# A Perceiver layer on one core: a written order for the prologue, helpers moved off VectorE, and a shorter last routing

## The chip, the cores and the metric

The kernel runs on one core of a Trainium2 chip. Its engines are TensorE (PE: matmuls and transposes), VectorE (DVE), ScalarE (ACT: activation functions from loaded tables), GpSimd (POOL) and SyncE (SP: issues DMAs). Each has its own in-order instruction stream; they synchronise by semaphores. The metric is the device time of one execution in microseconds. Kernel before: median 3076.52 us of three runs (3073.73 to 3076.61).

## The reference

Two batches of 512 tokens by 512 features (x), and two contexts of 8192 rows by 384 features. All arithmetic is in fp32.

```python
x = x + cross_attention(layernorm(x), ctx, mask, Wq, Wk, Wv, Wo)   # 16 heads of 32, 8192 keys, softmax
x = x + self_attention(layernorm(x), ...)   # 16 heads, causal, scores from amplitude and phase:
#   amp = softplus(x @ Wamp.T), normed by its root mean square in each head; phi = pi * tanh(x @ Wphi.T)
#   scores = (q_amp cos(q_phi) . k_amp cos(k_phi) + q_amp sin(q_phi) . k_amp sin(k_phi)) / sqrt(32) * exp(scale)
x = x + ffn(layernorm(x))                   # 16 experts, each token goes to its top 2
#   probs = softmax(x @ w_router); top_k(probs, 2); each expert takes 64 tokens of a batch at most, in the
#   order: all first choices by token, then all second choices; later ones are dropped
#   y = sum over the two choices of prob * w_proj(silu(w_gate x) * w_fc x)
```

An equal score goes to the lower expert number in the choice.

## The kernel before

**Cross-attention** is most of the time. Keys are taken in chunks of 1024 (8 a batch, 16 in all), heads in four groups of four. One chunk and one group is a *step*: 64 steps, each of eight *rounds* (one for each 128 keys, `kt`). A round on PE is: the scores of four heads for the row maxima of a later step (`heads_max`, L375, `LEAD` = 12 rounds ahead), the same scores with keys on partitions for the exponentials (`heads_exp`: L388 and the bias product L407), and one further piece: in even rounds the products with the values of the two rounds before (`values`, L440), in odd ones a piece of the keys two steps on (`k_half`) or a v tile of the next chunk (`v_tile`), both through `columns` (L166: 128 columns as four products of 32, side by side on the array). DVE takes the four maxima of 512 scores (L397), and adds products to the accumulator (L453, L455). ACT takes the four exponentials (L409), copies v tiles, the maxima as rows (`max_rows`, L431). POOL adds the exponentials of the step up to one tile (`es`, L570), from which PE makes the sums of the softmax (L467). When the running maximum moves, `shrink` scales the accumulator (L462, L463).

**Before the steps**, `prepare` (L239 to L328) loads the weights and the mask, computes layer norm of x for both batches (`norm_pieces`, L93 to L127), transposes it (`turn`, L139 and the copy L140), projects the queries (L310, 128 columns wide) and gathers the first masked column of the context for what the code calls the first keys (L283, L321). Its operations are left to a scheduler, and so is their order. Then a written order (`tc.manual_schedule()`, L493) holds: the k halves of steps 0 and 1, twelve rounds of maxima with the eight v tiles of chunk 0, row maxima, and the loop over steps (L514 to L584). `sa_tables` (L951 to L967), small tables for the self-attention, are made in step 1.

**When a batch ends** (step 32 is the first of batch 1), the last group's accumulator is divided by its sums in `divide` (L476 reciprocal, L477 product) on DVE, and `finish_tile` (L479 to L484) multiplies each of four token tiles by Wo and adds it to x. For other groups the product of `divide` is on POOL.

**During the last six steps**, `xattn_tail` (L881) gives out pieces of the self-attention of batch 0: norm (steps 58, 59), transposes, phases, amplitudes. One of them goes into each round: PE's into a free PSUM bank (`fill`), DVE's at the round's end (`fill_dve`). Tanh (L1235) and Sin (L1031) of the phases, and the square roots and logarithm of the amplitudes, are on ACT. The self-attention and the experts form a second `manual_schedule` (L1355); what lies between the two written blocks has its place by dependencies.

**Routing** (`route`, L645 to L760) gives 20 pieces: statistics and norm of the tokens, storing them to DRAM, transposes, router product (L679), softmax and two choices (L686 to L704), running counts of tokens for each expert (L710 to L725), rank and slot (L730 to L733), `hit` and `whose` (L734, L741), and a product that turns them into the list of tokens of each expert (L750, L753). For batch 0 they are spread over the self-attention of batch 1. For batch 1 they stand at the end (L1343 to L1350): after the last output tile nothing else is left for PE. Then `experts`: for each of 16, POOL fetches 128 rows by an indirect DMA (L767), PE transposes, expands (L788) and contracts (L805); results go to DRAM and are gathered back for each token (L833).

Of the kernel before, what the change touches and what calls it, by code (L numbers as in the profile page):

```python
# [42 lines left out]
def perceiver_kernel(ctx: ExitStack, tc: tile.TileContext, a, out: bass.AP):  # L43
# [33 lines left out]
    for b in range(B):  # L77
        nc.sync.dma_start(xs[:, b * TB : (b + 1) * TB, :], x_in[:, b * TB : (b + 1) * TB, :])
# [12 lines left out]
    lnp = ctx.enter_context(tc.tile_pool(name="ln", bufs=2))  # L91

    def norm_pieces(b, keep=None):  # L93
# [27 lines left out]

        class Tiles(list):
# [3 lines left out]
        pieces = [lambda i=i: stats(i) for i in range(TB)] + [scale] + [lambda i=i: normed(i) for i in range(TB)]  # L126
# [49 lines left out]
    def cross_attention(tail):  # L176

        with ExitStack() as st:
# [17 lines left out]
            def load_chunk(i):  # L196
                b, c = chunks[i]
                t = [m4("ctx", (P, CH)) for j in range(NC)]
                src = a["ctxT"][b].rearrange("(c p) k -> p c k", p=P)
                for j in range(NC):  # L200
                    nc.sync.dma_start(t[j], src[:, j, c * CH : (c + 1) * CH])
                m8 = sm.tile([P, CH], U8, tag="m8", name="m8")
                row = a["mask_BxS2_bf1"][b : b + 1, c * CH : (c + 1) * CH]
                nc.sync.dma_start(m8, row.to_broadcast([P, CH]))
                ctx_tiles[i], mask_tiles[i] = t, m8
# [3 lines left out]
            for w, n in ((wk, "Wk"), (wv, "Wv")):  # L209
                for j in range(NC):  # L210
                    nc.scalar.dma_start(w[j], a[f"L0_xattn_{n}"][j * P : (j + 1) * P, :])
            wo = b8("wo")
            nc.scalar.dma_start(wo, a["L0_xattn_Wo"].rearrange("(c p) d -> p c d", p=P))
            load_chunk(0)
# [24 lines left out]
            def prepare():  # L239

                with tc.tile_pool(name="xa_q", bufs=1) as qp:
                    wq = b8("wq")
                    nc.scalar.dma_start(wq, a["L0_xattn_Wq"].rearrange("(c p) d -> p c d", p=P))
                    mc8 = qp.tile([P, B, M // P], U8, name="mc8")
                    nc.gpsimd.dma_start(mc8, a["mask_BxS2_bf1"].rearrange("b (p n) -> p b n", p=P))

                    left_i = qp.tile([P, M // P], I32, name="left_i")
                    nc.gpsimd.iota(left_i, pattern=[[-1, M // P]], base=M, channel_multiplier=-(M // P))
                    left = qp.tile([P, M // P], F32, name="left")
                    nc.vector.tensor_copy(left, left_i)  # L250
                    val = qp.tile([P, B, M // P], F32, name="val")
                    nc.vector.tensor_tensor(
                        val, left.unsqueeze(1).to_broadcast([P, B, M // P]), mc8, ALU.mult
                    )
                    vm = qp.tile([P, B], F32, name="vm")
                    nc.vector.tensor_reduce(vm, val, AX.X, ALU.max)
                    pm = bank()
                    pf = bank()
                    nc.tensor.transpose(pm[:B, :P], vm, ident)
                    vb = qp.tile([B, 1], F32, name="vb")  # L260
                    nc.vector.tensor_reduce(vb, pm[:B, :P], AX.X, ALU.max)
                    dg = qp.tile([B, B], F32, name="dg")
                    nc.vector.tensor_scalar(dg, ident[:B, :B], vb, None, ALU.mult)
                    nc.tensor.matmul(pf[:, :B], ones[:B, :], dg, start=True, stop=True)
                    first = qp.tile([P, B], F32, name="first")
                    nc.vector.tensor_scalar(first, pf[:, :B], -1.0, float(M), ALU.mult, ALU.add)
                    nc.vector.tensor_scalar_min(first, first, M - 1.0)
                    anyb = qp.tile([P, B], F32, name="anyb")
                    nc.vector.tensor_scalar_min(anyb, pf[:, :B], 1.0)

                    at = qp.tile([P, B], F32, name="at")
                    rows = qp.tile([P, 1], F32, name="rows_at")
                    nc.vector.tensor_scalar(rows, iota_p, float(M), None, ALU.mult)
                    nc.vector.tensor_scalar(at, first, rows, None, ALU.add)
                    at_i = [qp.tile([P, 1], I32, name=f"at_{i}") for i in range(NC * B)]
                    cf1 = [qp.tile([P, 1], F32, name=f"cf_{i}") for i in range(NC * B)]
                    cf = qp.tile([P, NC, B], F32, name="cf")
                    table = a["ctxT"].rearrange("b c (k o) -> (b c k) o", o=1)
                    for i in range(NC * B):
                        nc.vector.tensor_scalar(  # L280
                            at_i[i], at[:, i % B : i % B + 1], float((i % B * CD + i // B * P) * M), None, ALU.add
                        )
# [6 lines left out]
                        nc.vector.tensor_copy(cf[:, i // B, i % B : i % B + 1], cf1[i])  # L289

                    is_bias = qp.tile([P, 1], F32, name="is_bias")
                    eq = qp.tile([P, 1], F32, name="is_row")
                    for j in range(4):
                        nc.vector.tensor_scalar(
                            eq if j else is_bias, iota_p, 32.0 * j + 3.0, None, ALU.is_equal
                        )
                        if j:
                            nc.vector.tensor_tensor(is_bias, is_bias, eq, ALU.add)
                    nc.vector.tensor_scalar(kmul, anyb, is_bias, BIG, ALU.mult, ALU.mult)
                    nc.vector.tensor_scalar(eq, is_bias, -1.0, None, ALU.add)  # L300
                    nc.vector.tensor_scalar(kadd, kmul, -1.0, eq, ALU.mult, ALU.add)

                    for b in range(B):
                        xnT = b8("xnT")
                        for i, xn in enumerate(norm_tiles(b)):
                            turn(Bank(bank()), "j", xn, xnT[:, :, i * P : (i + 1) * P], nc.scalar.copy)
                        for g in range(NG):
                            pq = bank()
                            for c in range(ND):
                                nc.tensor.matmul(  # L310
                                    pq,
                                    wq[:, c, g * P : (g + 1) * P],
                                    xnT[:, c, :],
                                    start=(c == 0),
                                    stop=(c == ND - 1),
                                )
# [162 lines left out]
            def finish_tile(b, acc, qt, po, after=None):  # L479
# [3 lines left out]
                if after:  # L483
                    after(qt)  # L484

            prepare()

# [902 lines left out]
```

## Time and profile before

| | |
|---|---|
| median of three runs | 3076.52 us (3073.73 to 3076.61) |
| profiled execution, its own time | 3074.43 us |
| its span | 3072.4 us |
| busy: PE / DVE / ACT / POOL | 2925.5 / 2027.4 / 1391.5 / 2167.0 us |
| mean granted PE clock | 0.978 |
| first exponential of step 0 | 117.58 us |
| steps 3 to 28 and most others | 37.11 us each |
| step 1; 32; 33 | 42.32; 57.0; 40.05 us |
| steps 58; 59 | 44.93; 46.22 us |
| last output matmul to first fetch | 2909.66 to 2932.08 us |

The page lists busy time and shares, then the chain of work that ended last: followed back from the last instruction, each time to what released it. A row of the chain has the start, the length, the engine and the line. A row of a timeline has start, length, engine, line, operation, output and inputs with their shapes and the number of instructions; in brackets stands the idle time of the engine ahead of it and what ended that. The name behind the arrow is the instruction that released it by the trace. A granted clock of 1.00 is full speed of PE. The length of a step is the distance between its first exponential and that of the next step.

### The profile page before, as it was taken

The numbers are of one execution on the slowest core, as the hardware profiler recorded it, in microseconds if no ns is written. First come the engines' busy times: TensorE is split into PE (matmuls) and PEld (weight loads), VectorE is DVE, ScalarE is ACT, GpSimd is POOL, SyncE is SP. The second block draws the span as 40 slices with busy tenths as digits, with TensorE's granted clock in tenths as the row PEclk, the third lists the DMA queues.
The fourth block names the chain that finished last, engine by engine and source line by source line (L and its number), as shares of the span: only waits on it lengthen the run. The fifth ranks groups of instructions, "written<-read, shape, count | busy, mean of one in ns | idle before, by whom it ended". The sixth has DMA issues, their size and how long they took to land.

```text
span 3072.4 us, 63904 instructions
## 1 busy us (share of the span) xinstructions
PE 2925.5 (95%) x27551; PEld 1128.2 (37%) x27551; DVE 2027.4 (66%) x3434; ACT 1391.5 (45%) x2597; POOL 2167.0 (71%) x861
## 2 busy tenths in 40 slices
PE   7999999999999999999999999999998998989875
PEld 3333333333333333333333333333332332334564
DVE  2667777776777677766777677677777656667522
ACT  1345554545455554535455555545554446352311
POOL 1388889898989898969888888888887752010112
PEclk9999999999999999999999999999999999999988
DMA  3000000000000000000000000000000001011274
GB/s 141 1 3 15 10 15 10 15 10 18 7 24 1 24 1 24 2 21 17 9 16 10 15 10 15 16 16 3 1 1 28 1 29 70 1 42 36 95 251 142
DMA packets 47371, 89.62 MB, mean 29 GB/s; under 512 B 4320, under 2 KB 22768, under 8 KB 47088
## 3 DMA queue, kind: packets, MB, share of 16 engines
q1 hardware_dynamic: 39824, 69.26, 7.0%
q0 software_dynamic: 2784, 8.41, 0.9%
q10 hardware_dynamic: 4480, 7.87, 0.8%
q8 instruction: 216, 3.54, 0.5%
q14 instruction: 67, 0.55, 0.1%
HBM read 77.13 MB, written 8.39 MB: 28 GB/s over the span
## 4 chain that ended last, share of the span: by engine, by line
PE 90%; DVE 6%; ACT 1%; DMA 1%; issue 1%; POOL 0%; ACTq 0%; POOLq 0%; DVEq 0%
PE s L166 30%; PE s L375 17%; PE s L440 16%; PE s L388 14%; PE s L407 3%; PE ph L788 2%; PE s L1062 2%; PE s L467 2%; PE s L310 1%; PE po L805 1%; DVE cm L397 1%; PE s L1144 1%; PE s L1183 1%; DMA wq<-in_L_xattn_Wq_dram 1%; DVE acc L476 1%
## 5 line engine op out<-in xcount | busy, mean ns | idle before, releaser
L570 POOL TENSOR_TENSOR es<-es,e 128x2048 f32<-128x2048 f32 x374 | 1700.2, 4546 | 80.1 <-ACT e L409 63.1
L409 ACT ACTIVATE e<-s 128x512 f32<-128x512 f32 x2048 | 1057.5, 602 | 1116.1 <-PE s L407 1113.1
L397 DVE TENSOR_REDUCE cm<-s 128x1 f32<-128x512 f32 x2048 | 1270.0, 682 | 315.8 <-PE s L375 315.7
L375 PE MATMUL s<-k,qT 32*128 32x512 f32 x4096 | 591.4, 640 | 3.7 <-DVE cm L397 3.7
L388 PE MATMUL s<-qT,k 32*128 32x512 f32 x4096 | 555.5, 595 | 7.6 <-ACT e L409 6.8
L440 PE MATMUL s<-e,v 128*32 128x512 f32 x4096 | 498.1, 604 | 12.6 <-DVE cm L397 11.4
L570 POOL TENSOR_TENSOR es<-e 128x2048 f32<-128x2048 f32 x63 | 286.1, 4542 | 226.7 <-ACT e L409 226.7
L166 PE MATMUL s<-wkv,ctx 128*32 128x512 f32 x3072 | 369.8, 602 | 7.5 <-DVE cm L397 7.2
L166 PE MATMUL s<-ctx,wkv 128*32 128x512 f32 x3072 | 357.2, 599 | 3.5 <-DVE cm L397 3.1
L388 PEld LDWEIGHTS s<-qT,k 32*128 32x128 f32 x4096 | 282.8, 185 | 188.2 <-issue 104.2
L455 DVE TENSOR_TENSOR acc<-acc,s 128x512 f32<-128x512 f32 (+1 forms) x359 | 207.7, 604 | 141.4 <-PE s L440 140.8
L375 PEld LDWEIGHTS s<-k,qT 32*128 32x128 f32 x4096 | 164.5, 183 | 333.7 <-issue 256.9
L440 PEld LDWEIGHTS s<-e,v 128*32 128x32 f32 x4096 | 107.6, 109 | 333.5 <-DVE cm L397 171.6
L407 PE MATMUL s<-rows,mb 4*128 4x512 bf16 x2048 | 217.9, 377 | 0.0
L351 DVE SCALAR_TENSOR_TENSOR k<-s,kf,m 128x512 f32<-128x512 f32 x128 | 96.1, 751 | 178.1 <-PE s L166 178.1
L166 PEld LDWEIGHTS s<-ctx,wkv 128*32 128x32 f32 x3072 | 87.4, 110 | 239.4 <-issue 156.2
L166 PEld LDWEIGHTS s<-wkv,ctx 128*32 128x32 f32 x3072 | 87.3, 110 | 224.6 <-issue 130.3
L366 ACT COPY v<-s 128x512 f32<-128x512 f32 x128 | 75.0, 586 | 119.7 <-PE s L166 96.8
L463 DVE TENSOR_TENSOR acc<-acc,s 128x1024 f32<-128x1024 f32 x56 | 68.4, 1221 | 70.0 <-ACT s L462 70.0
L1104 POOL TENSOR_TENSOR rest<-scm,parts 128x16 f32<-128x16 f32 x8 | 2.0, 256 | 155.5 <-DVE parts L1102 155.5
L1131 POOL TENSOR_SCALAR_AFFINE_SELECT e<-e 128x512 f32<-128x512 f32 x32 | 21.3, 677 | 128.2 <-ACT e L1129 128.2
L407 PEld LDWEIGHTS <-mb 4*128 4x128 bf16 x2048 | 68.2, 93 | 106.2 <-issue 105.5
(244 smaller groups left out, 1965.0 us busy)
## 6 DMA issues: line engine op xcount, KB each, us to landing
ctx<-in_ctxT_dram SPq DMA_DIRECT2D x48, 512.0 KB, 3.7
wg<-in_L_ffn_w_gate_dram SPq DMA_DIRECT2D x16, 512.0 KB, 4.7
wf<-in_L_ffn_w_fc_dram SPq DMA_DIRECT2D x16, 512.0 KB, 5.1
wp<-in_L_ffn_w_proj_dram SPq DMA_DIRECT2D x16, 512.0 KB, 5.4
results<-res ACTq DMA_DIRECT2D x32, 128.0 KB, 3.3
xs<-in_x_dram SPq DMA_DIRECT2D x2, 1024.0 KB, 6.6
m<-in_mask_BxS_bf_dram SPq DMA_DIRECT2D x16, 128.0 KB, 3.1
w_wq_phiT<-in_wq_phiT_dram SPq DMA_DIRECT2D x2, 1024.0 KB, 5.1
```

The lines of the kernel that those rows point to most:

```text
L166: nc.tensor.matmul(out[q], lhsT[:, q], rhs, start=start, stop=stop)
L351: nc.vector.scalar_tensor_tensor(k[:, keys], bank, kf[:, g, b : b + 1], mask_tiles[i][:, keys], ALU.subtract, ALU.mult)
L366: nc.scalar.copy(v[:, kt % (NKT // 2), :], bank)
L375: nc.tensor.matmul(s, qT(chunks[i][0], g, r, slice(qt * P, (qt + 1) * P)), k_tiles[n][r, hf * S : (hf + 1) * S], start=True, stop=True,)
L388: nc.tensor.matmul(s, k_tiles[n][r, keys], qT(chunks[i][0], g, r, slice(0, S)), start=True, stop=False)
L397: nc.vector.tensor_reduce(cms[g][chunks[i][1] % 2][:, qt, j : j + 1, hf], ss[j], AX.X, ALU.max)
L407: nc.tensor.matmul(ss[j], bias_tiles[i][r4, keys], rows[r4, :], start=False, stop=True)
L409: nc.scalar.activation(e[:, j, :], ss[j], AF.Exp)
L440: nc.tensor.matmul(av[j * HD : (j + 1) * HD, :], v_tiles[i][kt // (NKT // 2)][:, kt % (NKT // 2), h * HD : (h + 1) * HD], e[:, j, :], star ...
L455: nc.vector.tensor_tensor(dst, dst, src, ALU.add)
L463: nc.vector.tensor_tensor(acc[g], acc[g], pa.unsqueeze(1).to_broadcast([P, 2, S]), ALU.mult)
L570: nc.gpsimd.tensor_tensor(es, first if kt == 1 else es, e, ALU.add)
```

## The change

1. *Prologue.* `prepare` is written out in an order and stands in one `manual_schedule` that lasts to the end of the kernel. x of batch 0 is loaded as four tiles, first on SP; the mask for the search and Wq (in four pieces) come first on ACT's queue, then Wk, Wv; SP goes on with mask and chunk 0 (each array in two halves), x of batch 1, chunk 1, and Wo, which was on ACT. Queries go through `columns`. Only query (0, 0), the first keys of batch 0 and the keys of step 0 come before the twelve rounds of maxima; the rest is spread between them, `sa_tables` included.
2. *Division.* `inverse` (reciprocal, DVE) is apart from `divide` (product), which is on POOL also at the change of batch; output tiles are made in rounds 5 (one) and 7 (two) of step 32 and 1 of step 33.
3. *Norm of self-attention batch 0.* Adding epsilon and the Newton step (but for the reciprocal) are on POOL, the normalisation is an ACT `Identity` with scale and bias.
4. *One order from the first to the last instruction.* Where Tanh, Sin and some operations of the amplitudes stood among the last exponentials in the built order, they now stand after them.
5. *Routing.* The choices are made on exponentials, the probabilities come last; counts are sums by matmul in place of DVE's running sums; rank and position are made for both choices at once. For batch 1 a new `in_line` norms, transposes and routes three token tiles, and then the fourth; ACT does the first three normalisations.

The order within the steps, the loads of later weights, and the experts' code are as before. Cut to its core:

```diff
-            def prepare():
+            def prepare(qp):
+                for i in range(TB):
+                    nc.sync.dma_start(xs[:, i, :], x_in[:, i, :])
+                nc.scalar.dma_start(mc8, a["mask_BxS2_bf1"].rearrange("b (p n) -> p b n", p=P))
+                for c in range(ND):
+                    nc.scalar.dma_start(wq[:, c, :], a["L0_xattn_Wq"][c * P : (c + 1) * P, :])
...
+                load_chunk(0, 2)
+                nc.sync.dma_start(xs[:, TB:, :], x_in[:, TB:, :])
+                load_chunk(1)
+                nc.sync.dma_start(wo, a["L0_xattn_Wo"].rearrange("(c p) d -> p c d", p=P))
...
+                for i in range(TB):
+                    pieces[5 + i]()
+                    turned(0, tiles, i)
+                query(0, 0)
+                first_keys(0)
...
+                beside = [
+                    [q(0, 1)],
+                    [lambda: keys_of(1, 0), more["first"]],
+                    [lambda: keys_of(1, 1)],
+                    [v[0], v[1]],
+                    [q(0, 2)],
+                    [v[2], v[3]],
+                    [q(0, 3)],
+                    [v[4], more["turn"]],
+                    [q(1, 0)],
+                    [v[5], q(1, 1)],
+                    [v[6], q(1, 2)],
+                    [v[7], q(1, 3)],
+                ]
...
-                            qt = (kt - 3) // 2 if kt > 1 else 3
-                            if ending and (g == 0 and qt < 3 or g == 1 and qt == 3):
-                                finish_tile(b - 1, ending, qt, free.pop(0))
...
+                            for qt in {(0, 5): [0], (0, 7): [1, 2], (1, 1): [3]}.get((g, kt), []):
+                                finish_tile(b - 1, ending, qt, free.pop(0) if free else maxed[2])
...
+                    if ending and g == 0 and 3 <= kt < 7:
+                        divide(NG - 1, kt - 3, ending)
...
-                            divide(steps[n - 1][1], kt - 2, nc.vector if ending else nc.gpsimd, ending)
...
+                        inverse(steps[n - 1][1], kt - 2)
+                        if not ending:
+                            divide(steps[n - 1][1], kt - 2)
...
+        def newton():
+            nc.vector.reciprocal(rstd, t)
+            for out, x, y in ((t, rstd, rstd), (t, t, v)):
+                nc.gpsimd.tensor_tensor(out, x, y, ALU.mult)
+            nc.gpsimd.tensor_scalar(t, t, -0.5, 1.5, ALU.mult, ALU.add)
+            nc.gpsimd.tensor_tensor(rstd, rstd, t, ALU.mult)
+            nc.gpsimd.tensor_tensor(less, mv[:, :, 0], rstd, ALU.mult)
+            nc.gpsimd.tensor_scalar(less, less, -1.0, None, ALU.mult)
...
-            sa.tiles, sa.norm = norm_pieces(0)
-            return [], sa.norm[:5]
+            sa.tiles, sa.norm = norm_pieces(0, aside=True)
+            return [], sa.norm[:7]
...
+        def top_first():
+            pl = banks["pl"][:, :, :E]
+            nc.vector.tensor_reduce(mx[:, 0], pl, AX.X, ALU.max)
+            nc.vector.tensor_tensor(d, pl, over_e(mx[:, 0]), ALU.subtract)
+            nc.scalar.activation(pr, d, AF.Exp)
+            eq = tile("eq_0", [P, TB, E])
+            nc.vector.scalar_tensor_tensor(eq, d, 0.0, over_t(mo.falling), ALU.is_equal, ALU.mult)
+            first(0, eq)
...
-        def counted():
-            nc.vector.tensor_copy(so_far[:, :, 0, :], oh[:, :, 0, :])
-            for i in range(1, TB):
-                nc.vector.tensor_tensor(so_far[:, :, i, :], so_far[:, :, i - 1, :], oh[:, :, i, :], ALU.add)
+        def counted(k):
...
+            if k == 1:
+                for i in range(TB):
+                    nc.tensor.matmul(
+                        pp[:, 1], ones, oh[:, 0, i : i + 1, :].to_broadcast([P, TB, E]), start=(i == 0), stop=False
+                    )
+            nc.tensor.matmul(pp[:, k], mo.before, oh[:, k], start=(k == 0), stop=False)
+            for i in range(1, TB):
+                nc.tensor.matmul(pp[:, k, i:], ones, oh[:, k, : TB - i], start=False, stop=(i == TB - 1))
...
+        def in_line(output, between):
+            last = TB - 1
+            for i in range(TB):
+                output(i)
+                tiles.stats(i)
+                between(i)
+                if i == last - 1:
+                    tiles.scale_of(0, last)
+                    for j in range(last):
+                        tiles.scaled(j)
+                        stored(j)
+            turn(ps, pstag, tiles[0], mxnT[:, :, :P], nc.scalar.copy)
+            tiles.scale_of(last, TB)
+            for j in range(1, last):
+                turned(j)
+            tiles.normed(last)
+            stored(last)
+            router(range(last))
...
+            turn(ps, pstag, tiles[last], mxnT[:, :, last * P :], halves)
+            router([last])
+            for f in found:
+                f()
+            nc.scalar.activation(tile("warm", [P, 1]), eps, AF.Sigmoid)
```

## The prediction

> **What bounds it now.** I read the page first: TensorE (PE) is busy 2925.5 of 3072.4 us, and the chain that ended last is PE's.
>
> ```profile
> PE 90%; DVE 6%; ACT 1%; DMA 1%; issue 1%; POOL 0%; ACTq 0%; POOLq 0%; DVEq 0%
> ```
>
> So only two things can pay: PE work that goes, and places where PE stands still. In steady state nothing is to be had: the first exponential of one step follows that of the step before at 37.11 us in nearly all of the 64 steps, PE is busy throughout, and the built order of those steps is the same in both kernels on every engine. Listing the first exponentials gives the exceptions: step 1 takes 42.32 us, step 32 57.0, step 33 40.05, steps 58 and 59 44.93 and 46.22; the first one comes at 117.58. Outside the steps are the end of cross-attention, the last routing and the experts. I take these in turn.
>
> The chain of waits over the prologue:
>
> ```profile
> 9.47 18.29 DMA wq<-in_L_xattn_Wq_dram
> 27.90 16.26 PE s L310 x32
> 47.81 13.84 PE s L310 x32
> 104.03 9.05 DVE cm L397 x15
> ```
>
> Wq, issued last on ACT's queue, lands at 27.8; all eight queries stand ahead of the first key; and at the end maxima of VectorE (DVE) run alone, after which PE starts slow (timeline of PE):
>
> ```profile
> 113.12 2.68 PE L375 MATMUL s<-k,qT 32*128 32x512 f32 x8 [2.73 <-DVE cm L397]
> ```
>
> The same eight matmuls take 1.14 elsewhere; the granted clock is 0.83 in 100 to 120 us.
>
> **A, prologue.** Removed: the wait for Wq. After the change four 256 KB tiles of x lead SP's queue, and the small mask and Wq lead ACT's; all x landed at 7.4 before, and it is no further back now. Then DVE: last tile's statistics 0.9, variance to 1/sqrt about 1.5 (the six rows at 16.34 to 19.4 without their gaps), four normalisations of 0.54, with transposes (2.82 for 12) and copies of 0.59 behind them: the first query starts near 15.6 instead of 27.90. ACT's eleven issues (0.39 to 0.63 each) end near 6, ahead of its Sqrt, so they hide; Wv, ctx, second x and Wo come later than their data is needed by 5 us or more at the 338 GB/s of the first 20 us; Wo on SP is wanted 1300 us later. From 15.6 PE has this list to the end of the twelve lead rounds: eight queries of 3.46 (13.84 for four) 28, plus 3 for the first at the slow start that 16.26 against 13.84 shows; first keys 2 x 3.3 (12 wide matmuls took 2.8; now 48 narrow ones each batch: an estimate, 2.8 to 4.5); four key halves 10.4; twelve rounds of maxima 1.0 each, 12; eight v tiles 2.71 each, 21.7; transposes 2 and row maxima 0.4. Sum 84, ending at 99.6. DVE's work beside it (48 reductions of 0.62, 30 us; four key copies 3; second norm 7; small ones 5) is 45 and hides, where it was the end before. First exponential 2.2 later, at 101.8: gain 15.8. POOL's six gathers (1.25 apart) start when the mask is known, near 11 instead of 18.19; three serve the first keys, land 6 us later, near 20, just as query 0 ends. Step 1's excess of 5.2 goes too: there the tables of the self-attention cost
>
> ```profile
> 160.89 3.65 DVE L963 TENSOR_SCALAR mine<-hsc 32x4 f32<-32x4 f32 x4
> 165.91 3.46 PE s L440 x16
> ```
>
> and they now sit in lead round 6, where PE has 2.7 to 3.6 of other work for each round. A = 21. Ends: 27 if x arrives tile by tile and nothing is cold, 14 if Wq still takes its 18.29 from issue to landing (query at 20) and 3 us of cold PE remain.
>
> **B, batch switch (steps 32, 33).** Together 97.05 against 2 x 37.11 and four output tiles of 3.57 (wo rows): 8.5 lost. Timelines of DVE, PE and POOL:
>
> ```profile
> 1322.31 2.92 DVE L477 TENSOR_TENSOR acc<-acc 128x128 f32<-128x128 f32 x1
> 1325.88 4.48 PE L166 MATMUL s<-ctx,wkv 128*32 128x512 f32 x24 [3.10 <-DVE cm L397]
> 1320.56 9.12 POOL L570 TENSOR_TENSOR es<-es,e 128x2048 f32<-128x2048 f32 x2 [0.39 <-ACT e L409]
> ```
>
> The division's multiply takes 2.92 while POOL adds, ending as POOL's first addition ends; alone it takes 0.29. The maxima behind it on DVE are late, PE waits 3.10 and then runs 4.48 for 2.78. Four multiplies go to POOL (0.45 each, 1.8 in a step that has 47.8 us for POOL's 34); DVE keeps the reciprocal (0.95, not lengthened in its rows). On POOL the multiply waits behind an addition of up to 4.55, and the output tile is written one round or more later, so nobody waits. Two output tiles in one round leave ACT and DVE idle, not PE. B = 7; ends 4 (the second place stays) and 8.5.
>
> [...]
>
> **C, norm of self-attention batch 0 (steps 58, 59).** 44.93 + 46.22 − 74.22 = 16.9 over.
>
> ```profile
> 2318.37 4.42 DVE L106 TENSOR_SCALAR ln_v<-ln_mv 128x4 f32<-128x4 f32 x1
> 2324.68 5.24 PE L166 MATMUL s<-wkv,ctx 128*32 128x512 f32 x24 [4.74 <-DVE cm L397]
> 2344.11 0.54 DVE L117 TENSOR_SCALAR ln_xn<-xs,ln_mv,ln_r 128x512 f32<-128x512 f32 x1
> 2349.05 3.55 DVE L117 TENSOR_SCALAR ln_xn<-xs,ln_mv,ln_r 128x512 f32<-128x512 f32 x1
> 2353.25 3.37 PE L440 MATMUL s<-e,v 128*32 128x512 f32 x16 [2.72 <-DVE cm L397]
> ```
>
> Where POOL's addition began 0.1 to 1.3 us earlier, the same normalisation lasts 3.55 instead of 0.54, and PE loses the wait and the slow matmuls after it (3.37 for 1.92). After: normalisations are ACT activations near 0.6 in rounds where ACT rests 1.5 to 2.8; the small arithmetic is seven POOL instructions near 0.25, 1.8 on an engine with 3 us to spare a step. The added wait: Sqrt on ACT waits for POOL's small add behind an addition, and the next four exponentials stand behind it, with two table loads of 1.28 that were there before; ACT's rest of 2 does not hold all of 2.8 plus up to 4.5, so I leave 3. DVE's reciprocal waits for Sqrt with maxima queued behind it, but a round later. C = 14; ends 9 and 16.
>
> **D, end of cross-attention.**
>
> ```profile
> 2557.00 2.95 ACT L1031 ACTIVATE sn<-phi 128x1024 f32<-128x1024 f32 x3
> 2563.92 2.57 PE L388 MATMUL s<-qT,k 32*128 32x512 f32 x8 [6.75 <-ACT e L409]
> 2583.69 0.59 ACT L982 COPY v<-s 128x512 f32<-128x512 f32 x1 [9.97 <-PE s L166]
> ```
>
> Sin and four extra table loads stand among the last exponentials; PE waits 6.75, runs the next ones slow (about 3), and waits 1.00 to 1.17 three times. After, Tanh (3.9), a load (1.28) and Sin (4) follow the last exponential, in ACT's idle 9.97; one later reload goes (1.3). D = 9: 6.75 + 3 + 1.3, less 2 for Tanh that may outlast the gap. Ends 5 and 12.
>
> [...]
>
> **E, routing.** Last batch: PE's last output matmul ends at 2909.66, POOL's first fetch is issued at 2932.08, 22.4 later:
>
> ```profile
> 2913.51 3.53 PE L139 MATMUL s<-ident,xn 128*128 128x128 f32 x16 [3.89 <-DVE xn L117]
> 2929.26 1.86 PE L750 MATMUL s<-whose,hit 128*64 128x16 f32 x16 [2.36 <-DVE whose L741]
> ```
>
> Three tiles' normalisation, transposes and router now lie before or beside the fourth's, so after it come statistics 1.6, scale 1.5, xn 0.5, four transposes 0.9, copy 0.4, eight matmuls 0.95 and latencies: logits at 6.7 instead of 11.1. First choice 3.6 more (it contains a table load of 1.28 for Exp, which now waits behind Sqrt's table, about 0.85 of it exposed); second choice and counts, ranks, hit and numbers 4.7, since three rows of probabilities leave the path and the sums 0.82 become matmuls. Fetch at 15.7: E = 6.7, ends 5 and 8.5. The earlier routing gets nine more small matmuls in PE's stream (0.234 each, 2.1) and loses a wait of 2.27, but gets about 1 of new wait: −0.8, ends −2 and +1.
>
> **F, experts.** PE stands 6.3 in gaps that no semaphore explains, such as
>
> ```profile
> 2952.95 0.37 PE L788 MATMUL ph<-bT,wf 128*128 128x128 f32 x1 [2.35 <-issue]
> ```
>
> The change doesn't touch the code there. I take 0; it could go (+8) or grow (−3).
>
> **Sum.** 21 + 7 + 14 + 9 + 6.7 − 0.8 = 56.9 off the profiled execution's own 3074.43 us (span 3072.4): 3017.5. That execution lies 2.1 under the median of 3076.52, so 3018.5 stands between. All low ends together give 3042, all high ends 2994.
>
> **Rivals.** (1) The prologue pays little: first keys wait for gathers, or queries for Wq; A = 9, 3030. For it: the gathers' 6 us landing; against: only the first of eight needs to be early. 0.12. (2) The stall among the experts goes with the shifted fetches: 3010. Its cause isn't in the trace. 0.15. [...] 0.12. (4) Slower: the granted clock falls in the body, since PE has fewer rests. Each 0.01 of it is about 29 us over 2900 us of PE; at 0.978 − 0.02 the gain is gone, at 0.95 the time is 3098. Against it: stretches with 20 of 20 us busy show 1.00, and the low values follow rests. 0.05. (5) The change doesn't move the waits at all, within 6 us: 0.02.
>
> The forecast has 0.54. The range 2999 to 3040 takes in (1) to (3) and leaves out the slower case and both ends together. 0.2% is about 6 us, which is what a measurement of this kernel can tell: faster 0.92, within 0.03, slower 0.05.
>
> **What would show it.** First exponential near 102, step 1 at 37; steps 32 and 33 together near 90; 58 and 59 near 77; no wait of PE over 3 us at the last exponentials; fetch 16 us after the last output; steady steps at 37.11 still. I am wrong if exponentials in step 58 wait for POOL, if queries start after 20, or if the steady steps change.

## The result and the profile after

The changed kernel takes 3021.41 us (median of four, 3021.1 to 3023.5), the kernel before 3075.93 (median of four, beside it): a ratio of 0.9825, 95% interval 0.9808 to 0.9842, 54.5 us less. Its profiled execution took 3021.1 us, with a span of 3019.4 against 3072.4: 53.0 less. The prediction was 3018.5, in a range of 2999 to 3040.

The page's chain is still PE's:

```profile
PE 91%; DVE 5%; ACT 1%; issue 1%; POOL 1%; DMA 1%; ACTq 0%; POOLq 0%; DVEq 0%
```

Since both kernels have the same steps, the 53 us can be split by marks in the two traces (all in us; starts from the timelines, differences worked out):

| stretch | before | after | less | predicted |
|---|---|---|---|---|
| to the first exponential | 117.58 | 103.16 | 14.4 | 15.8 |
| step 1 | 42.32 | 36.62 | 5.7 | 5.2 |
| steps 32 and 33 | 97.05 | 88.60 | 8.4 | 7 |
| steps 58 and 59 | 91.15 | 75.87 | 15.3 | 14 |
| other steps up to the start of step 63 | 2176.04 | 2176.79 | −0.7 | 0 |
| start of step 63 to the square root of the second norm | 80.97 | 75.22 | 5.7 | 9 |
| from there to the last output product's end | 304.50 | 303.94 | 0.6 | −0.8 |
| from there to the first fetch | 22.47 | 18.69 | 3.8 | 6.7 |
| from there to the end | 140.3 | 140.5 | −0.2 | 0 |

Of the other steps, 61 and 62 are long as well (48.78 and 49.84 us, filled with self-attention); the prediction's list of exceptions leaves them out, and the change leaves their lengths alone.

The chain of waits over the prologue after the change; its columns are start, length and work:

```profile
3.76 6.92 DMA wq<-in_L_xattn_Wq_dram
14.27 3.99 PE s L193 x16
18.92 9.65 PE s L220 x138
```

Wq has landed at 10.7, 8 us ahead of the first query at 18.92. What ends last ahead of it is now the norm, and the transposes behind it run slow (3.31 us; the same sixteen take 1.97 later). In PE's timeline one wait is left in the lead rounds:

```profile
39.15 0.98 PE L220 MATMUL s<-cf,wkv 128*32 128x1 f32 x96 [2.15 <-DVE cf L378]
41.24 4.31 PE L220 MATMUL s<-ctx,wkv 128*32 128x512 f32 x24
```

The first keys of batch 1 wait for three small copies that stand on DVE behind four maxima, the statistics of the second norm and the scaling of the other keys (L425); the key products after that take 4.31 for the 2.78 of the same group ahead of it. These 48 narrow products cost 0.98, not the 3.3 that the prediction had.

In steps 32 and 58 the products and the small arithmetic are on POOL, each behind an addition; PE's longest wait in step 32 is 0.81 us (timelines of POOL and ACT):

```profile
1305.58 0.46 POOL L555 TENSOR_TENSOR acc<-acc 128x128 f32<-128x128 f32 x1
1305.99 4.53 POOL L680 TENSOR_TENSOR es<-es,e 128x2048 f32<-128x2048 f32 x1
2295.07 0.25 POOL L174 TENSOR_SCALAR ln_v<-ln_mv 128x4 f32<-128x4 f32 x1
```

```profile
2295.54 1.28 ACT L175 ACT_TABLE_LOAD   x1
2296.84 0.20 ACT L175 ACTIVATE ln_t<-ln_v 128x4 f32<-128x4 f32 x1
2297.06 1.28 ACT L483 ACT_TABLE_LOAD   x1
2298.35 2.06 ACT L483 ACTIVATE e<-s 128x512 f32<-128x512 f32 x4
```

POOL's epsilon is ready at 2295.32, ahead of ACT's Sqrt, so the wait that was feared there does not occur. Step 58 (38.70) is still 1.6 us longer than 37.11; the two table loads ahead of the exponentials are what the rows offer for it, and no run varied them, so that cause isn't shown.

At the end of cross-attention (PE's timeline) two waits of over 2 us remain, and the value products after them start slow, 8.60 where 7.07 was the length before:

```profile
2516.37 1.19 PE L462 MATMUL s<-qT,k 32*128 32x512 f32 x5 [2.31 <-ACT e L483]
2527.69 1.06 PE L541 MATMUL s<-es,ones 128*32 128x512 f32 x8 [2.44 <-POOL es L683]
2529.57 8.60 PE L220 MATMUL s<-w_wvT,sxnT 128*32 128x512 f32 x64 [0.81 <-DVE acc L529]
```

POOL's last addition, which the second wait is for, is itself held. It takes 3.34 us where most of those further up take 2.35 to 2.38, and it starts 0.10 us after VectorE's addition of the other half; the one ahead of it, 0.02 us behind VectorE's, takes 3.41 (timelines of DVE and POOL):

```profile
2524.19 1.23 DVE L683 TENSOR_TENSOR es<-es,e 128x1024 f32<-128x1024 f32 x1 [2.21 <-ACT e L483]
2524.30 3.34 POOL L683 TENSOR_TENSOR es<-es,e 128x1024 f32<-128x1024 f32 x1
```

In a second trace of the same kernel (`after_again`) POOL's addition starts 0.87 us ahead of DVE's; there POOL's takes 2.36 and DVE's 2.57. In these rows the one that starts first keeps its length.

In the last routing PE's timeline shows where the missing 3 us went:

```profile
2869.52 0.66 PE L845 MATMUL s<-oh,before 128*128 128x64 f32 x2 [1.44 <-DVE oh L804]
2869.97 1.41 PE L847 MATMUL s<-oh,ones 128*128 128x48 f32 x6
2871.22 1.95 PE L842 MATMUL s<-oh,ones 128*128 128x64 f32 x8
2872.96 0.63 PE L845 MATMUL s<-oh,before 128*128 128x64 f32 x2
2873.39 1.41 PE L847 MATMUL s<-oh,ones 128*128 128x48 f32 x6
2876.05 1.86 PE L876 MATMUL s<-whose,hit 128*64 128x16 f32 x16 [1.25 <-DVE hit L861]
```

DVE has the second choice at 2871.77, but the 24 records of the twelve count products occupy PE from 2869.52 to 2874.80, at 0.22 us each. The same products in the routing of batch 0 take 0.13 each (0.79 for 6), at a granted clock of 1.00 although PE waits 1.70 us ahead of them. In the windows of the trace the columns are the length, busy time and records of PE, PEld, DVE, ACT and POOL, then the granted clock:

```profile
2860.00:2867.00 7.00, 5.74 (x48) 4.78 (x44) 3.44 (x11) 4.21 (x8) 0.00 (x0) 1.00 0.48 172
2867.00:2868.00 1.00, 1.00 (x6) 0.96 (x5) 0.05 (x1) 0.00 (x0) 0.00 (x0) 0.60 0.89 317
2868.00:2878.00 10.00, 7.21 (x41) 6.98 (x40) 4.54 (x19) 3.02 (x4) 0.00 (x0) 0.50 0.33 112
```

From 2868 to 2878 the clock is 0.50, with no wait over 1.44 us. It has fallen already from 2867 to 2868, ahead of that wait; the longest wait since the last output product is 0.70.

### The profile page after: what moved, and what is told of

The parts are those of the page before. It is cut to its first block, busy times and chain, and to the rows that moved or that the text cites. A ratio compares the mean times of both kernels' runs of the same rounds, so it can differ in the third digit from the quotient of the medians.

```text
span 3019.4 us, 64707 instructions
## 1 busy us (share of the span) xinstructions
PE 2913.7 (96%) x27947; PEld 1120.3 (37%) x27947; DVE 2003.8 (66%) x3410; ACT 1390.4 (46%) x2602; POOL 2170.6 (72%) x872
## 4 chain that ended last, share of the span: by engine, by line
PE 91%; DVE 5%; ACT 1%; issue 1%; POOL 1%; DMA 1%; ACTq 0%; POOLq 0%; DVEq 0%
PE s L220 31%; PE s L449 17%; PE s L514 16%; PE s L462 14%; PE s L481 4%; PE ph L954 2%; PE s L1228 2%; PE s L541 2%; PE po L971 1%; PE s L1310 1%; PE s L1349 1%; DVE cm L471 1%; DVE acc L549 1%; POOL r L999 0%; DVE acc L529 0%
## 5 line engine op out<-in xcount | busy, mean ns | idle before, releaser
L425 DVE SCALAR_TENSOR_TENSOR k<-s,kf,m 128x512 f32<-128x512 f32 x128 | 96.1, 751 | 171.7 <-PE s L220 171.7
```

Of the source, the lines that this page charges most:

```text
L425: nc.vector.scalar_tensor_tensor(k[:, keys], bank, kf[:, g, b : b + 1], mask_tiles[i][:, keys], ALU.subtract, ALU.mult)
```

## The experiments

They ran on three chips, on which the kernel before took 3063 to 3067 us and not 3076. Each run is compared by the lengths of its steps, or with the runs beside it. Between the versions of the changed kernel, steps that a run leaves alone agree to 0.01 us, but for a few that differ by up to 0.29.

**Is it GpSimd that holds VectorE in steps 32, 58 and 59?** First, the work goes back to VectorE; then GpSimd's additions are left out as well.

```diff
-                        divide(NG - 1, kt - 3, ending)
+                        divide(NG - 1, kt - 3, ending, nc.vector)
...
-            sa.tiles, sa.norm = norm_pieces(0, aside=True)
-            return [], sa.norm[:7]
+            sa.tiles, sa.norm = norm_pieces(0)
+            return [], sa.norm[:5]
...
-            return [], sa.norm[7:]
+            return [], sa.norm[5:]
```

> The changed kernel with two things put back on VectorE: the four products of the batch switch (in the new rounds), and the whole norm of the self-attention's batch 0. Theory (VectorE stands still while GpSimd adds): step 32 from 48.6 back to 53 to 57 us, step 58 from 38.7 to 44.9, step 59 from 37.2 to 46.2, in all 19 to 24 us more. Rival (the rounds in which things are done paid, not the engine): step 32 stays at 48.6 and steps 58 and 59 together under 80.

Step 32 took 59.04 us, steps 58 and 59 44.61 and 46.04: 25.3 more than the changed kernel's three steps, a little above what the theory expected, and far from the rival. Step 32 is even longer than in the kernel before (57.0), so the new rounds are no gain by themselves. DVE's timeline:

```profile
1307.72 3.44 DVE L555 TENSOR_TENSOR acc<-acc 128x128 f32<-128x128 f32 x1
1326.33 0.29 DVE L555 TENSOR_TENSOR acc<-acc 128x128 f32<-128x128 f32 x1
2301.70 4.43 DVE L107 TENSOR_SCALAR ln_v<-ln_mv 128x4 f32<-128x4 f32 x1
2332.06 3.55 DVE L118 TENSOR_SCALAR ln_xn<-xs,ln_mv,ln_r 128x512 f32<-128x512 f32 x1
```

```diff
                     if kt == 0:
                         first = e
+                        if n in (32, 58, 59):
+                            es = e
+                    elif n in (32, 58, 59):
+                        pass
                     elif lead:
                         nc.gpsimd.tensor_tensor(es, first if kt == 1 else es, e, ALU.add)
```

> As the run before it (products and norm on VectorE), but GpSimd's additions of the exponentials are left out in steps 32, 58 and 59: the softmax sums of these steps take the first round alone. Theory (VectorE stands still only because GpSimd runs): products 0.29, epsilon 0.17 and normalisations 0.54 us each in the rows, step 32 at 48.6 to 49.6, steps 58 and 59 at 37 to 39.5. Rival (VectorE has no room for these instructions, or waits for Sqrt): the rows are short but steps 58 and 59 stay above 43.

Steps 32, 58 and 59 took 49.03, 38.26 and 37.11 us, with the same instructions on DVE in the same order:

```profile
1304.62 0.28 DVE L555 TENSOR_TENSOR acc<-acc 128x128 f32<-128x128 f32 x1
2288.59 0.16 DVE L107 TENSOR_SCALAR ln_v<-ln_mv 128x4 f32<-128x4 f32 x1
2312.66 0.54 DVE L118 TENSOR_SCALAR ln_xn<-xs,ln_mv,ln_r 128x512 f32<-128x512 f32 x1
```

So DVE has room for this work, and most of the 3.4 to 4.4 us in a row is the wait for POOL. That settles both parts.

**Which instructions are held?** A function `priced` issues one small instruction in each of three steps, on tiles of 128x4 that nothing else reads (128x64 in the last two groups).

```diff
+                    if kt == 4:
+                        priced(n)
                     if fill_dve:
                         fill_dve.pop(0)()
```

> The changed kernel with one instruction more in round 4 of three steps each, right after the place where GpSimd is given its addition: VectorE tensor_scalar (steps 8 to 10), tensor_reduce (12 to 14), tensor_tensor of two SBUF inputs (16 to 18), reciprocal (20 to 22), GpSimd tensor_scalar (24 to 26), VectorE copy (36 to 38), VectorE tensor_scalar of 64 (40 to 42), ACT Identity (44 to 46), all small. Theory: tensor_scalar, copy and tensor_tensor last up to 4.5 us and make their step 3 to 6 us longer; tensor_reduce, reciprocal, GpSimd's and ACT's last under 0.4 and leave the step at 37.1. Rival (any instruction more on VectorE there costs the same): all five forms of VectorE make the step longer alike.

No step changed, but this says nothing about the question. In the rows (operation, count: least, median and largest ns) nothing is held, and POOL's timeline shows why: one of its instructions ends at 418.27 and the next starts at 418.35, so the instruction at 418.26 fell between two of them.

```profile
L626 DVE TENSOR_SCALAR tiny<-tiny x3: 160/163/165, 418.3 to 492.5; 128x4 f32<-128x4 f32 x3
L630 DVE TENSOR_TENSOR tiny<-tiny x3: 154/154/156, 715.2 to 789.4; 128x4 f32<-128x4 f32 x3
```

The second try puts the call behind `heads_max` of round 6:

```diff
                         free = free[:2]
+                        if kt == 6:
+                            priced(n)
```

> As the run of prices, whose instructions fell between two of GpSimd's additions; now they are issued in round 6 right behind the four maxima, where the rows show GpSimd adding without a break. Theory (a VectorE instruction is held until the addition ends if it has two SBUF inputs or is a plain tensor_scalar or copy): tensor_scalar, copy and tensor_tensor last 1 to 4 us and their steps grow by 1 to 4; tensor_reduce and reciprocal stay under 0.3, their steps at 37.1. Rival (no form is held): all stay under 0.3 and every step stays at 37.1. Rival 2 (any form is held): all five last over 1 us.

```profile
L626 DVE TENSOR_SCALAR tiny<-tiny x3: 1668/1678/1684, 423.5 to 499.3; 128x4 f32<-128x4 f32 x3
L628 DVE TENSOR_REDUCE tiny<-tiny x3: 148/148/149, 574.3 to 648.6; 128x1 f32<-128x4 f32 x3
L630 DVE TENSOR_TENSOR tiny<-tiny x3: 1661/1674/1691, 722.8 to 798.6; 128x4 f32<-128x4 f32 x3
L632 DVE RECIPROCAL tiny<-tiny x3: 169/169/170, 873.6 to 947.9; 128x4 f32<-128x4 f32 x3
L636 DVE COPY tiny<-tiny x3: 1668/1678/1684, 1482.9 to 1558.7; 128x4 f32<-128x4 f32 x3
```

tensor_scalar, copy and the product of two SBUF inputs last 1.66 to 1.69 us, ten times the 0.16 and 0.15 of tensor_scalar and product in `prices`, and lengthen their steps by 0.77 to 0.81 us, a little less than the 1 to 4 that the theory expected; tensor_reduce (0.15) and reciprocal (0.17) are not held, and their steps stay at 37.1. The tensor_scalar of 128x64 is held too (1.71 us, steps 0.81 to 0.82 longer); the small instructions on POOL (0.22) and ACT (0.26) change no step. A held instruction costs its step less than it waits here (0.8 for about 1.5 us), so the step had about 0.7 us of slack there; the 4.4 us in step 58 are past that. The row of the reciprocal (0.17 us) says why `inverse` could stay on DVE.

**Is the order of Tanh and Sin the whole gain at the end of cross-attention?** The kernel before, with one written order from the first keys on.

```diff
             prepare()
+            ctx.enter_context(tc.manual_schedule())
...
-            with tc.manual_schedule():
+            if True:
...
-    with tc.tile_pool(name="mo_w", bufs=1) as mo_w, tc.manual_schedule():
+    with tc.tile_pool(name="mo_w", bufs=1) as mo_w:
```

> The kernel before, with nothing changed but that one written order holds from the first matmul of the keys to the end. Theory: the whole gain at the end of cross-attention comes from the place of Tanh and Sin: the wait of 6.75 us among the last exponentials goes, 5 to 6.5 us less in all, and every step keeps its length. Rival (the gain there comes from other edits): under 1 us.

3059.5 against 3066.95 us, ratio 0.9975 (0.9966 to 0.9985). From step 63 to the square root it takes 75.03 us; before it was 80.97 and after the change 75.22. The steps keep their lengths to within 0.17 us. So this part is the order alone: 5.9 of the 7.5 us that the run gained in all; where the rest lies is open. The same waits remain as in the changed kernel (2.31 for ACT's amplitudes between the exponentials, 2.44 for POOL's last addition).

**What paid in the prologue?** Two halves were undone, one at a time. In the first, queries, transposes, the second norm and keys are written out ahead of the rounds, and the rounds keep the v tiles.

```diff
                 beside = [
-                    [q(0, 1)],
-                    [lambda: keys_of(1, 0), more["first"]],
...
+                beside = [[v[t]] if t < NKT else [] for t in range(LEAD)]
```

> The changed kernel with all eight queries, the transposes of batch 1 and all keys of steps 0 and 1 ahead of the twelve rounds of maxima, as before; loads and their order are those of the changed kernel. Theory (part of the gain comes from spreading queries between the rounds, where VectorE would end the last four rounds alone): first exponential at 109 to 113 us instead of 103.2. Rival (only the early Wq paid): 102 to 105.

The first exponential is at 110.99 us; with the changed kernel's prologue it came at 100.2 to 104.5 in eight traces, two of them from the same set of runs (100.16 and 101.17). The chain shows DVE's maxima again:

```profile
88.65 2.76 PE s L220 x24
97.59 9.58 DVE cm L471 x16
```

Part of these 9.58 us is `sa_tables`, which stands in round 6 there too, with its 1.9 us of waiting for ACT.

```diff
                 wq = b8("wq")
-                for c in range(ND):
-                    nc.scalar.dma_start(wq[:, c, :], a["L0_xattn_Wq"][c * P : (c + 1) * P, :])
                 for w, n in ((wk, "Wk"), (wv, "Wv")):
...
+                nc.scalar.dma_start(wo, a["L0_xattn_Wo"].rearrange("(c p) d -> p c d", p=P))
+                nc.scalar.dma_start(wq, a["L0_xattn_Wq"].rearrange("(c p) d -> p c d", p=P))
```

> The changed kernel with Wo back on ScalarE's queue and Wq behind it, last, in one DMA. Theory (Wq's place in the queue paid): Wq lands at 20 to 25 us, the first query starts then instead of 18.9, and the first exponential comes 3 to 8 us later than 103.2. Rival (the norm ends last there, Wq would have been in time): the first query and the first exponential within 1 us of 18.9 and 103.2.

Wq lands at 22.93, PE waits 4.15 us for it and starts slow (4.94 for the first query's products, 3.64 for the second's); first exponential at 108.59.

```profile
11.22 11.71 DMA wq<-in_L_xattn_Wq_dram
23.06 10.94 PE s L220 x138
```

So both halves paid, 6.5 to 11 and 4 to 8 us (each run against the eight traces; 9.8 to 10.8 and 7.4 to 8.4 against the two of the same set), and neither alone. The second half is the place of Wq and its four pieces together; they were not tried apart.

**Why did the last routing give 3.8 us and not 6.7?** First, running sums on DVE (`sums`, one choice at a time) and three products (`summed`) take the place of the twelve.

```diff
         found = [
             top_first,
-            lambda: (counted(0), top_second()),
-            lambda: counted(1),
+            lambda: (sums(0), top_second()) if split else (counted(0), top_second()),
+            lambda: summed() if split else counted(1),
```

> The changed kernel with the counts of the last batch's routing as running sums on VectorE and three small products (as before) in place of twelve products; everything else in that routing stays. Theory (on a PE at half clock the 22 records of the twelve products, 5.3 us, end last there): the product of ranks starts 0.8 to 1.6 us sooner after the first choice, and the first fetch with it. Rival (VectorE's sums are the longer way): 0 to 1 us later.

From the first maximum of the logits to the first fetch: 9.54 us, against 10.77 in the changed kernel; 1.23 less. (The expectation's 22 records are 24.) The first choice's sums (0.17 and 0.59 us) hide in DVE's wait for the exponentials (0.89 in the changed kernel), and PE's products take 1.65 us:

```profile
2869.41 0.77 PE L898 MATMUL s<-oh,before 128*128 128x128 f32 x2 [3.84 <-DVE oh L804]
2869.98 0.72 PE L901 MATMUL s<-sofar,ones 128*128 128x96 f32 x2
2870.48 0.58 PE L902 MATMUL s<-sofar,ones 128*128 128x64 f32 x2
```

The other way is to bring PE's clock up again; `spin(2)` stands ahead of the list of tokens, `spin(10)` behind it:

```diff
+            idle = ps1.tile([P, S], F32, tag="j", name="idle")
+
+            def spin(n):
+                for _ in range(n):
+                    nc.tensor.matmul(idle[:, :256], ones, xs[:, 0, :256], start=True, stop=True)
+
+            spin(1)
             router([last])
+            spin(3)
...
+            spin(10)
```

> The changed kernel with 16 products that nothing reads (256 columns, 0.43 us each at full clock) in PE's waits of the last routing: one ahead of the fourth tile's router product, three behind it, two ahead of the list of tokens, ten while the first fetch lands. Theory (the clock falls in these waits and makes the counts and the first expert slow): granted clock from 0.50 to over 0.85 between the fourth router product and the first expert; the 22 records of the counts take 2.5 to 3.5 us instead of 5.3, the first expert's gate products 1.95 instead of 3.3 to 3.7; 2.5 to 4.5 us less from the last output to the second expert. Rival (the slow rows are not a matter of the clock, or the added products come in the way): 0, or up to 2 us more.

The counts take 3.0 us, the first expert's gate products 2.05, and from the fourth tile's neighbours (the start of the twelve transposes) to the second expert it is 25.63 us; the changed kernel in the same set of runs has 29.53. 3.9 us less, of which 1.9 lie ahead of the first fetch. (The whole time of this single run, 3010.08, can't show that: the changed kernel's own runs beside it go from 3007.9 to 3013.3.) PE's timeline:

```profile
2872.84 1.08 PE L842 MATMUL s<-oh,ones 128*128 128x64 f32 x8
2873.76 0.39 PE L845 MATMUL s<-oh,before 128*128 128x64 f32 x2
2883.83 2.05 PE L967 MATMUL ph<-bT,wg 128*128 128x128 f32 x16 [0.26 <-DVE bT L194]
```

The windows of the two traces give 0.83 for 0.54 from 2868 to 2878 us, and 1.00 for 0.50 from 2878 to 2885. But the idle products did not keep the clock from falling. The first two of these windows are of `pe_warm`, the third of the changed kernel beside it (`after_again`):

```profile
2864.00:2868.90 4.90, 4.87 (x42) 4.41 (x40) 1.77 (x7) 1.66 (x5) 0.00 (x0) 1.00 0.62 207
2868.90:2872.30 3.40, 3.40 (x13) 2.86 (x12) 1.93 (x9) 2.46 (x3) 0.00 (x0) 0.50 1.06 374
2868.70:2889.00 20.30, 12.36 (x65) 11.73 (x65) 6.98 (x28) 3.02 (x4) 7.01 (x8) 0.50 0.52 166
```

In both the clock falls near 2868.8, in `pe_warm` after 4.9 us of which PE is busy, by its records, 4.87. With products of 256 columns behind that it is back after 3.4 us, without them after 20.3. So the theory holds for the low clock that lasts, and not for the fall, which came in `pe_warm` without a wait. Whether the narrow router products and transposes ahead of it bring it, or something else, no run varied. From the last output product to the fall, no wait of PE is over 0.70 us in either trace.

**The kernel itself again, and two versions with the repairs.**

> The changed kernel itself, on the chip of these experiments, to compare with the kernel before and with the run after it. Both theories: 0.982 to 0.985 of the kernel before; if the gaps among PE's first experts belong to the chip and not to the kernel, neither kernel shows them here and the difference stays 50 to 55 us.

3010.02 us against 3067.22, ratio 0.9815 (0.9798 to 0.9831). PE's gaps among the first experts (6.3 us before, 5.4 after, in the first comparison) are in none of the traces of the experiments: from the second expert's gate products to the end it takes 119.5 to 121.5 us there, and 128.7 and 129.0 in the two traces of the first comparison.

```diff
-                    [q(0, 1)],
-                    [lambda: keys_of(1, 0), more["first"]],
+                    [q(0, 1), more["first"]],
+                    [lambda: keys_of(1, 0)],
...
-                    [v[7], q(1, 3)],
+                    [q(1, 3), v[7]],
...
-                    for f in norm[:2]:
-                        f()
-                    del norm[:2]
+                    if t > 1:
+                        for f in norm[:2]:
+                            f()
+                        del norm[:2]
...
+                nc.scalar.activation(qp.tile([P, 1], F32, name="warm"), eps, AF.Sqrt)
...
+                idle = bank()
+                for _ in range(7):
+                    nc.tensor.matmul(idle[:, :256], ones, xs[:, 0, :256], start=True, stop=True)
...
-                    else:
+                    elif t + 1 < total:
                         for eng, u in ((nc.gpsimd, slice(0, 2)), (nc.vector, slice(2, 4))):
...
-            add_sums(len(steps) - 1, sums, slice(0, S), bank())
+            add_sums(len(steps) - 1, sums, slice(0, S), bank(), waiting[-1][2])
```

The activation stands between the issues of Wq and Wk, and `add_sums` takes the last tile of exponentials as a second product. The sums of `counts_dve` are in it, and `spin` 1, 8, 2 and 10 times.

> The changed kernel with all that the runs suggest: first keys of batch 1 in lead round 0 and the second norm from round 2 on, the last query ahead of the last v tile, Sqrt's table loaded between the issues of Wq and Wk, seven idle products ahead of the first transposes; counts of the last batch on VectorE; idle products in the last routing; the softmax sums of the last step taken from seven additions and the last tile by PE, without GpSimd's last addition. Theory: first exponential 4 to 8 us sooner, 1 to 2 at the end of cross-attention, 3 to 5 at the last routing: 8 to 14 us less than the changed kernel. Rival (the waits only move): under 4 us less.

3000.5 us, ratio to the kernel before 0.9785 (0.9769 to 0.9801): 9.5 us less than the changed kernel beside it. The prologue gives most of it: the first exponential is at 96.46 against 104.49. Its four edits were not run apart, so what each is worth isn't shown. The other two did not give what was expected. From step 63 to the transposes it takes 380.9 us against 380.0. From there to the second expert it takes 27.31, more than `pe_warm` alone: eight idle products last 6.14 us, where the ten behind the list of tokens take 4.58, and end after the second choice.

```profile
7.51 6.27 PE L342 MATMUL s<-xs,ones 128*128 128x256 f32 x14
13.62 1.91 PE L193 MATMUL s<-ident,ln_xn 128*128 128x128 f32 x16
2862.16 6.14 PE L954 MATMUL s<-xs,ones 128*128 128x256 f32 x16
```

```diff
-            spin(8)
+            spin(4)
...
-            add_sums(len(steps) - 1, sums, slice(0, S), bank(), waiting[-1][2])
+            add_sums(len(steps) - 1, sums, slice(0, S), bank())
```

> The run best without its change to the last softmax sums, and with four idle products behind the fourth router product in place of eight (the eight lasted 6.1 us there and ended 1 to 2 us after the second choice was known). Theory (both were losses in best): from the last exponentials' step to the transposes of the last routing 380.0 us as in the changed kernel instead of 380.9, from these transposes to the second expert's gate products 25 to 26 us instead of 27.3, in all 2 to 3 us less than best against the kernel before. Rival (chance of the clock, not these edits): within 1 us of best.

From the transposes to the second expert: 25.1 us, as expected. From step 63 to the transposes: 380.5, and in the other runs with the changed kernel's end 379.0 to 380.3, so the sums' change is neither a gain nor a loss that these runs can show. In time it can't be told from `best`, and the 2 to 3 us less that were expected against the kernel before do not show: 3001.76 us, ratio 0.9791 (0.9777 to 0.9805), with spans of 3000.0 and 3002.1 in the profiled executions. Both beat both kernels.

## Why the prediction was right, point by point

- **What bounds it.** Right: the steps that the change does not touch keep their lengths to within 0.01 us, but for steps 0, 25 and 26, which are 0.08 to 0.21 longer, and all gains are places where PE stood still.
- **A, prologue.** 20.1 of the predicted 21, by errors that nearly cancel; that the sum comes out so close is luck. The first query came at 18.92 and not 15.6: ACT's DMA issues lasted until 11.03 and not 6 (three for Wk took 4.16), so Sqrt's table load started at 11.07 and DVE waited 1.15 for it, x's third tile came at 7.92, and the transposes were slow (3.31 for 1.97). The list on PE took 81.3 (18.92 to 100.21) instead of 84: first keys 0.98 each instead of 3.3, no slow first query, but one new wait of 2.15 with slow products after it (4.31 for 2.78).
- **B and C, the switch of batches and the norm.** Right in mechanism, which `lock_back`, `lock_free` and `prices_mid` show, and slightly low in size: 8.4 for 7, because one wait of 0.81 is all that is left; 15.3 for 14, because Sqrt never waited for POOL, and only the table loads stayed (two of 1.28 us).
- **D, end of cross-attention.** Right in mechanism (`one_order`), too high in size: 5.7 for 9. The term that failed is "6.75 + 3 + 1.3, less 2": of the 6.75, 2.31 remain for ACT's amplitudes between exponentials, and POOL's last addition (2.44) now ends last ahead of the sums, and the value products behind it start slow (8.60 for 7.07). Of that addition's 3.34 us about 1 is the wait behind VectorE's. The 2 for Tanh were not lost: after Sin, ACT waits 1.67 for PE.
- **E, routing.** 3.8 for 6.7. The prediction's own terms, 6.7 + 3.6 + 4.7, add to 15.0, and not to the 15.7 that it goes on with. The first failed term is the logits, at 7.9 after the last output instead of 6.7: DVE waits 0.87 for a Sqrt that stands on ACT behind normalisations and a copy, and the fourth tile's transposes stand on PE behind the router products of the other three. The first choice is known 1.3 after the logits, and not 3.6. The second failed term is "counts ... 4.7": from the first choice to the fetch it takes 9.5, since the sums that leave DVE became 24 records on a PE at a granted clock of 0.50, 5.3 us. `counts_dve` puts 1.2 and `pe_warm` 1.9 us on that. The load of Exp's table costs the second choice 0.89 us, but PE's counts end after it. In batch 0 nothing was lost.
- **F, experts.** Taken as 0, and 0 it was, as both kernels of the first comparison have the gaps. That they are missing in other runs of the same program was not foreseen.

The sum, 56.9, against 53.0 in the spans: A to C 1.8 too low, D and E with the earlier routing 4.8 too high, other steps 0.7.

## What to carry to other kernels

Look at where the bounding engine stands still, place by place; the lengths of equal steps give each place's worth to 0.1 us before anything is changed. A small instruction that lasted ten times its usual length while another engine ran (1.67 us for 0.16) was waiting here, not working, and moving it to that other engine's own queue removed the wait, since the engine had room (in step 32 PE's longest wait went from 3.10 to 0.81 us). Where a latency chain passes through PE in small products, count them at the slow clock (here 0.22 us each at 0.50, 0.13 at 1.00), or give PE something idle to do (3.9 us less in `pe_warm`), but only as much as fits into the wait (the eight products of 6.14 us in `best` did not).

## What the runs showed that was not expected

- Which VectorE operations were held while GpSimd added is sharp: 1.67 us for tensor_scalar, copy and a two-input product of 128x4, 0.15 and 0.17 for reduce and reciprocal at the same place; and the tensor_scalar that fell between two of GpSimd's was not held (0.16). GpSimd is held in turn: its addition took 3.34 us for 2.35 when VectorE's began first.
- PE's clock fell to 0.50 after at most 0.70 us of waiting, and with idle products in the waits after 4.9 us with 4.87 busy. Products of 256 columns in the waits brought it back after 3.4 us instead of 20.3. What makes it fall there stays open.
- The gaps of PE among the first experts are in both traces of the first comparison (from the second expert on 128.7 and 129.0 us) and in none of the twelve traces of the experiments (119.5 to 121.5), which come from three chips. What causes them stays open; no run here varied it.
